# An attention and expert layer on one core: the output projection multiplied out earlier, small loads on another queue, norms, first front and maxima moved in the order

## The chip, the cores and the metric

The kernel runs on one core of one Trainium2 chip, in one launch. The metric is the device time in microseconds (us), the median of the runs. A core has a matrix engine (TensorE, in the profile PE, with its weight loads as PEld), a vector engine (VectorE, DVE), an activation engine (ScalarE, ACT), a general engine (GpSimd, POOL) and a sync engine (SyncE, SP) that here only issues DMAs. Every engine runs its own instructions in the order of the program and waits for the others by semaphores.

## The reference, cut to what matters

The input is 8 batches of 512 tokens of width 128, in f32. Two sublayers, each with a norm before and after, and a residual:

```
x = x + layernorm(attention(layernorm(x)))     # 1 head of 128, rotary, causal
x = x + layernorm(ffn(layernorm(x)))
# ffn(x):
h = rmsnorm(x, g1); c = h @ w_down             # 128 -> 64
q, k, v = rope(c @ wq), rope(c @ wk), c @ wv   # 16 heads of 4, causal softmax
x = x + attn @ w_up
t = rmsnorm(x, g2)
gate = top-2 of softmax(t @ router_w), 8 experts
y = sum_e gate_e * (silu(t @ w1_e) * (t @ w3_e)) @ w2_e     # all 8 experts computed
return x + y
```

The first attention has one head as wide as the model, the second has sixteen heads of width 4.

## The kernel before, in words

**Stages.** The program is one long order, written out by hand with generators: `yield` marks the places where pieces of two tasks are put side by side, and `step` advances a task by one piece. There are three stages: the wide attention (the first sublayer, batch by batch, to about 133 us), then the sixteen-headed attention in "units" of four heads (four units a batch, 32 in all), and the experts, from 441 us on. The next stage's first pieces are already mixed into the last batches of the stage before.

**The wide attention.** `wide_attention` goes through b = 0 to 8. In loop b it works on three batches at once: `norm` and `turn` of batch b + 1, `project`, `values` and `scores` of batch b, `turn_probs` and `weigh` of batch b - 1. It yields four times in a loop, so the i-th yield lies in loop i // 4. By engine:

- ACT: `norm` writes `xn` from `x_all` with a scale and shift of POOL's (L245); `turn` copies `xnT` from the matrix engine's bank (L256); `scores` takes exponentials into `p` (L299); `turn_probs` copies `pT` (L320); `values` copies `v` (L280).
- PE: `turn` transposes `xn` (L199), `project` makes `pq` (L262, one for q and one for k), `scores` makes `sc` in two halves with a mask added (L291, L292), `turn_probs` transposes `p` into `pT_ps` (L317), `values` makes `pv` (L272) and `weigh` makes `pr` (L327).
- DVE: two products `two` with the rotary table (L264), the row maxima `nmax` (L297), `h_all` (L336), the statistics of `x` (`stats_x`, tiles `bnst_x`), of the result (`norm_result`, `bnst_r`), the add of the normed result to `x_all` (`add`, L350), the statistics of that sum (`norm_sum`, `bnst_h`).
- POOL: the rotary sum `roped` (L266), which `scores` needs, the reciprocal roots (L169) and shifts.

`norm_result`, `add` and `norm_sum` run inside the loop for batches 0 to 2 (`CLOSED = 3`); the other batches' run later, by `close`.

On-chip accumulators: three double banks (`wide`, for `pq`, `sc`, and later `pqk`, `sm`, `sT`, `ph`) and, in this stage, two single banks (`bank`) that every transposition, `pv` and `pr` take by turns. A transposition into a bank waits until the copy of what was in it two turns before is done.

**Output projection.** Since the weights are fixed, `fuse_projections` multiplies `wv` by `wo` once, into `wvo`, and takes the row mean out of it, so that `values` gives values that are projected already: a transposition of `wv`, ACT's copy `wvT`, a product, three small DVE steps.

**Preparation.** `prepare` makes `wg` and `wqk4` from the second sublayer's small weights and turns its rotary table; `fill` writes constants and pads. They are stepped in loops 0 to 2 (list `setup`).

**The first front.** `ffn_front(b)` prepares batch b for the sixteen heads: POOL scales `x_all` into `hs` (L462), PE turns it into `hT_ps` (L199), then `pqk` (L534) and `pvs` (L546), a rotary product (L542) and sum `rot`, and POOL splits the result into three bf16 parts, `thirds` (L451 to L455). Six DMAs write them to DRAM (`q_dram`, `k_dram`, L569), and `load_rows` reads them back in another layout, `q_rows` and `k_rows`, with four DMAs (L577). For batches 0 and 1 SyncE issues these DMAs (`queue`). The front of batch 0 (list `first`) is stepped in loops 3 and 4, two pieces at a yield; that of batch 1 (list `fronts`) later, one piece at a time.

**Maxima.** Before a unit's weights can be computed, `rowwise` makes its scores by rows (`sm`, L617 and masks L600) and `highest` takes their maxima (`nm`, L632): six such blocks a unit, then POOL splits them into `m`, PE turns them (`m3T`, L650) and SyncE's six DMAs put them into `q_rows` (L658). `columnwise` then makes the scores by columns (`sT`, L673). `period(n)` is the order of one unit's time; it works on the maxima of unit n + 2. The maxima of units 0 and 1 are made in `period(-2)` and `period(-1)` (list `units_begin`, fourteen pieces), which are stepped in the last loops of the wide attention.

Of the kernel before, what the change touches and what calls it, by code (L numbers as in the profile page):

```python
# [8 lines left out]
F32 = mybir.dt.float32  # L9
BF16 = mybir.dt.bfloat16  # L10
# [5 lines left out]
P = 128  # L16
# [6 lines left out]
def kernel(  # L23
# [22 lines left out]
    nc = tc.nc  # L46
    B, T, D = x.shape
    NT = T // P
    L = w_down.shape[1]
    H, HD, HP = 16, 4, 32  # L50
# [3 lines left out]
    E, _, F = w1.shape  # L54
# [4 lines left out]
    const = ctx.enter_context(tc.tile_pool(name="const", bufs=1))  # L59
# [7 lines left out]
    def banks(stack, **bufs):  # L67

        for name, n in bufs.items():
            psum[name] = stack.enter_context(  # L70
                tc.tile_pool(name=f"ps_{name}_{n}", bufs=n, space=bass.MemoryType.PSUM)
            )
# [4 lines left out]
    def bank(name):  # L77
        return psum["bank"].tile([P, 512], F32, tag="bank", name=name)
# [3 lines left out]
    for b in range(B):  # L82
        nc.sync.dma_start(
            out=x_all[:, b * NT : (b + 1) * NT, :],
            in_=x[b].rearrange("(t p) d -> p t d", p=P),
        )
        if b == 0:
            ropea = const.tile([P, 2, T], F32, name="ropea")
            nc.sync.dma_start(out=ropea, in_=rope_a)


    wqk = const.tile([P, 2, 2, D], F32, name="wqk")
    for i, w in enumerate((a_wq, a_wk)):
        nc.scalar.dma_start(out=wqk[:, i, 0, :], in_=w[0])
        nc.scalar.dma_start(out=wqk[:, i, 1, 0 : D // 2], in_=w[0][:, D // 2 : D])
        nc.scalar.dma_start(out=wqk[:, i, 1, D // 2 : D], in_=w[0][:, 0 : D // 2])
    wv = const.tile([P, D], F32, name="wv")
    nc.scalar.dma_start(out=wv, in_=a_wv[0])
    wo = const.tile([P, D], F32, name="wo")
    nc.scalar.dma_start(out=wo, in_=a_wo[0])  # L100

    w1s = const.tile([P, E, F], F32, name="w1s")
    w3s = const.tile([P, E, F], F32, name="w3s")
    w2s = const.tile([P, E, FC, D], F32, name="w2s")
    for s in range(2):
# [4 lines left out]
            out=w2s[:, es, :, :], in_=w2[es].rearrange("e (c f) d -> f e c d", f=P)  # L110
# [71 lines left out]
    def ln_stats(src, n0, tag, n=NT):  # L182

        mv = moments(src, n0, tag, n)
        ve = stat.tile([P, n], F32, tag="ve", name=f"ve_{tag}_{n0}")
        nc.vector.tensor_scalar(ve, mv[:, :, 1], EPS, None, ALU.add)  # L186
        return mv, root(ve, tag)
# [20 lines left out]
    def fuse_projections():  # L208
        ps = bank("wvo_ps")
        nc.tensor.transpose(ps[:, :P], wv, ident)  # L210
        wvT = work.tile([P, D], F32, tag="sq", name="wvT", bufs=1)
        nc.scalar.copy(wvT, ps[:, :P])
        ps = bank("wvo_ps2")
        nc.tensor.matmul(ps[:, :P], wvT, wo, start=True, stop=True)
        mean = stat.tile([P, 1], F32, tag="wvo_mean", name="wvo_mean", bufs=1)
        nc.vector.tensor_reduce(mean, ps[:, :P], AX.X, ALU.add)
        nc.vector.tensor_scalar(mean, mean, 1.0 / D, None, ALU.mult)
        nc.vector.tensor_scalar(wvo, ps[:, :P], mean, None, ALU.subtract)

    def minus_product(a, b, tag, name):  # L220
        d = stat.tile([P, b.shape[1]], F32, tag=tag, name=name)
        nc.gpsimd.tensor_tensor(d, a, b, ALU.mult)
        nc.gpsimd.tensor_scalar(d, d, -1.0, None, ALU.mult)
        return d
# [3 lines left out]
    def stats_x(b):  # L228
        mv, rstd = ln_stats(x_all, b * NT, "x")
        x_stats[b] = minus_product(mv[:, :, 0], rstd, "shift_x", f"shift_x_{b}"), rstd  # L230
# [151 lines left out]
            h_scale[b] = kept  # L382

    batches = [Wide(b) for b in range(B)]
    with tc.manual_schedule():
        stats_x(0)
        batches[0].norm()
        stats_x(1)


    wdown = const.tile([P, L], F32, name="wdown")
    nc.gpsimd.dma_start(out=wdown, in_=w_down)
    wqkv = const.tile([L, 3, L], F32, name="wqkv")
    for i, w in enumerate((f_wq, f_wk, f_wv)):
        nc.gpsimd.dma_start(out=wqkv[:, i, :], in_=w)
    wup = const.tile([L, D], F32, name="wup")
    nc.gpsimd.dma_start(out=wup, in_=w_up)
    wr = const.tile([P, E], F32, name="wr")
    nc.gpsimd.dma_start(out=wr, in_=router_w)
    g1c = const.tile([P, 1], F32, name="g1c")  # L400
    nc.gpsimd.dma_start(out=g1c, in_=g1.rearrange("(p o) -> p o", o=1))
    g2c = const.tile([P, 1], F32, name="g2c")
    nc.gpsimd.dma_start(out=g2c, in_=g2.rearrange("(p o) -> p o", o=1))
    ropef = const.tile([P, NT, 2, HD], F32, name="ropef")
    nc.gpsimd.dma_start(out=ropef, in_=rope_f.rearrange("(t p) s d -> p t s d", p=P))
    ident_bf = const.tile([P, P], BF16, name="ident_bf")
    nc.vector.tensor_copy(ident_bf, ident)

# [3 lines left out]
        out=mask_a,  # L412
        in_=mask_a,
# [4 lines left out]
        channel_multiplier=1,  # L418
    )

    def half_masks(name, sign):


        m = const.tile([P, 2, P], BF16, name=name)
        nc.gpsimd.memset(m, 0.0)
        for i in range(2):
            for h in range(2):
                at = m[i * HR : (i + 1) * HR, h, :]
                nc.gpsimd.affine_select(
                    out=at,  # L430
                    in_=at,
                    compare_op=ALU.is_ge,
                    fill=NEG_BF,
                    base=sign * HR * h,
                    pattern=[[-sign, P]],
                    channel_multiplier=sign,
                )
        return m

    mask_q = half_masks("mask_q", -1)  # L440
    mask_k = half_masks("mask_k", 1)

    order = const.tile([P, E], F32, name="order")
    for e in range(E):
        nc.gpsimd.memset(order[:, e : e + 1], float(E - e))


    def split(thirds, x, r):
# [477 lines left out]
    fronts, backs, later = [], [], []  # L926

    def step(tasks):
        while tasks:
            try:  # L930
                next(tasks[0])
                return True
            except StopIteration:
                tasks.pop(0)
# [64 lines left out]
    def wide_attention():  # L999
        for b in range(B + 1):  # L1000
            u = batches[b] if b < B else None
            nxt = batches[b + 1] if b + 1 < B else None
            v = batches[b - 1] if b > 0 else None
            w = batches[b - 2] if 0 <= b - 2 < CLOSED else None
            if nxt:
                nxt.norm()
            if w:
                w.norm_result()
            if u:
                u.project(0)  # L1010
            if v:
                v.turn_probs(0, 1)
            if u:
                u.project(1)
            yield
            if b == 0:
                fuse_projections()
            if v:
                v.turn_probs(2)
                v.turn_probs(3)  # L1020
            if w:
                w.add()
            if u:
                u.values()
            if w:
                w.norm_sum()
            yield
            if v:
                v.weigh()
            if b + 2 < B:  # L1030
                stats_x(b + 2)
            if nxt:
                nxt.turn()
            if u:
                u.scores(0)
            yield
            if u:
                u.scores(1)
            yield

    def front_and_rows(b):
        yield from ffn_front(b)
        yield
        load_rows(b)

    CLOSED = 3
    setup = [prepare(), fill()]
    first = [front_and_rows(0)]
    units_begin = [period(-2), period(-1)]
    begun = period(0)  # L1050
    with tc.manual_schedule():
        banks(ctx, wide=3)
        with ExitStack() as stage:
            banks(stage, bank=2)
            batches[0].turn()
            fronts.append(front_and_rows(1))
            for i, _ in enumerate(wide_attention()):
                b = i // 4
                if b < 3:
                    step(setup)  # L1060
                    step(setup)
                elif b < 5:
                    step(first)
                    step(first)
                else:
                    step(first)
                    step(fronts)
                    if b > 5 or i % 4 > 1:
                        step(units_begin)
            for _ in range(6):  # L1070
                step(fronts)
                step(units_begin) or next(begun)
    closes = [batches[b].close() for b in range(CLOSED, B)]
    banks(ctx, bank=1, po=1)
    with tc.manual_schedule():
# [20 lines left out]
    for i, engine in enumerate((nc.gpsimd, nc.vector)):  # L1096
        n0, at = (B - 1) * NT + i * NH, slice(i * NH, (i + 1) * NH)
        st = ln_stats(h_all, n0, "o", NH)
        for t in range(NH):
# [3 lines left out]
            out=out[B - 1].rearrange("(t p) d -> p t d", p=P)[:, at, :], in_=y[:, at, :]  # L1103
# [71 lines left out]
```

## Time and profile before

| what | before |
|---|---|
| median of 3 runs | 798.55 us (798.25 to 801.8) |
| the profiled execution's own time | 799.5 us |
| its span, first to last instruction | 797.7 us |
| mean granted TensorE clock | 0.986 |
| PE busy | 726.2 us, 91% of the span |
| DVE, ACT, POOL busy | 490.3, 325.7, 285.1 us |
| DMA | 30.36 MB |

All times are those of one execution, taken by the profiler. A line of a timeline gives the start, the length, the engine, the program's line, the operation, the tile written and the tiles read, how many instructions were merged, and in brackets how long the engine was idle before it and what ended the idle time. SPq, ACTq and POOLq are the issue of DMAs. A line of the waits gives who waited for whom, the total in us, how many times, and the longest. A line of the windows gives the stretch, its length, the busy time of PE, PEld, DVE, ACT and POOL, the granted clock, the share of the DMA engines and GB/s. Matrix products run in a pipeline and their ends are modelled, so start-to-start distances are used for sums.

### The profile page before, as it was taken

How to read it: one execution, taken by the hardware profiler on the slowest of the kernel's cores; microseconds unless marked ns; L12 is line 12 of the kernel's file. 1: busy time of each engine (PE TensorE's matmuls, PEld its weight loads, DVE VectorE, ACT ScalarE, POOL GpSimd, SP SyncE). 2: the span in 40 equal slices, each digit the busy share in tenths (PEclk: the TensorE clock that was granted, in tenths of full speed). 3: DMA queues.
4: the chain of work that ended last, by engine and by line, in shares of the span. 5: the costliest groups of instructions: out<-in, count | busy, mean ns of one | idle time of the engine just before them, and what ended most of it. 6: DMA issues, size and time to landing. Idle time of an engine off the chain costs nothing. (4 is left out here: it accounts for less than half of the span.)

```text
span 797.7 us, 15024 instructions
## 1 busy us (share of the span) xinstructions
PE 726.2 (91%) x5886; PEld 433.0 (54%) x5886; DVE 490.3 (61%) x1090; ACT 325.7 (41%) x507; POOL 285.1 (36%) x595
## 2 busy tenths in 40 slices
PE   4989897898989889998899898999999999999995
PEld 2657465444445444544444455666666666666663
DVE  3587667788878777768672244746454545454554
ACT  2553533565656556656567323222222222222221
POOL 7576450456868676757424030101010101010101
PEclk9999999999999999999999899999999999999998
DMA  9121304040312122313000000000000000000000
GB/s 277 41 88 36 84 11 111 18 107 3 97 27 85 39 62 64 93 31 103 22 3 3 0 1 1 14 1 14 1 14 1 14 0 14 1 14 0 14 1 13
DMA packets 29017, 30.36 MB, mean 38 GB/s; under 512 B 6164, under 2 KB 25332, under 8 KB 28948
## 3 DMA queue, kind: packets, MB, share of 16 engines
q0 software_dynamic: 5280, 14.31, 7.0%
q1 hardware_dynamic: 22516, 14.72, 6.5%
q8 instruction: 46, 0.75, 0.4%
q10 hardware_dynamic: 1152, 0.39, 0.2%
q14 instruction: 23, 0.19, 0.1%
HBM read 15.73 MB, written 11.53 MB: 34 GB/s over the span
## 5 line engine op out<-in xcount | busy, mean ns | idle before, releaser
L632 DVE TENSOR_REDUCE nm<-sm 128x2 f32<-128x1024 f32 (+2 forms) x192 | 194.2, 1042 | 35.5 <-PE sm L600 30.6
L696 ACT ACTIVATE pk<-sT 128x1024 f32<-128x1024 f32 x160 | 161.2, 1024 | 78.5 <-PE sT L600 78.0
L874 ACT ACTIVATE sil<-ph 128x512 f32<-128x512 f32 x128 | 76.3, 597 | 248.4 <-PE ph L866 228.1
L875 DVE TENSOR_TENSOR hid<-sil,ph 128x512 f32<-128x512 f32 x128 | 87.2, 686 | 139.0 <-ACT sil L874 138.9
L887 PEld LDWEIGHTS py<-w2s,hid 128*128 128x128 f32 x1016 | 124.1, 193 | 33.4 <-issue 28.7
L866 PE MATMUL ph<-tT_all,w1s 128*128 128x512 f32 x256 | 131.9, 597 | 0.0
L866 PE MATMUL ph<-tT_all,w3s 128*128 128x512 f32 x256 | 131.1, 593 | 0.0
L887 PE MATMUL py<-w2s,hid 128*128 128x128 f32 x1016 | 125.2, 277 | 4.0 <-DVE o_nat L730 2.0
L169 POOL TENSOR_TENSOR root_o<-ve_o,half 128x4 f32<-128x4 f32 (+1 forms) x9 | 8.6, 951 | 295.4 <-DVE ve_o L186 259.9
L703 PE MATMUL po<-pk,vpad 128*32 128x512 f32 (+3 forms) x1024 | 97.8, 444 | 0.0
L896 DVE SCALAR_TENSOR_TENSOR h_all<-py,gate_all,h_all 128x128 f32<-128x128 f32 x254 | 71.7, 344 | 34.5 <-PE py L887 34.5
L866 PEld LDWEIGHTS ph<-tT_all,w3s 128*128 128x128 f32 x256 | 48.9, 191 | 61.8 <-issue 61.8
L673 PE MATMUL sT<-q_rows,k_rows 64*128 64x384 bf16 (+3 forms) x512 | 64.9, 299 | 18.2 <-DVE nm L632 13.8
L617 PE MATMUL sm<-k_rows,q_rows 61*128 61x256 bf16 (+3 forms) x512 | 71.1, 305 | 5.5 <-ACT pk L696 3.5
L866 PEld LDWEIGHTS ph<-tT_all,w1s 128*128 128x128 f32 x256 | 44.1, 192 | 31.7 <-issue 21.2
L617 PEld LDWEIGHTS <-q_rows 61*128 61x128 bf16 x512 | 23.5, 94 | 56.2 <-issue 52.1
L600 PE MATMUL sm<-ident_bf,mask_q 64*128 64x64 bf16 (+1 forms) x768 | 49.2, 200 | 0.0
L600 PEld LDWEIGHTS <-mask_q 64*128 64x128 bf16 x768 | 38.9, 96 | 12.0
L600 PE MATMUL sT<-ident_bf,mask_k 64*128 64x128 bf16 (+1 forms) x640 | 43.6, 206 | 0.0
L673 PEld LDWEIGHTS <-k_rows 64*128 64x128 bf16 x512 | 26.2, 93 | 31.6 <-issue 31.0
L451 POOL CAST m<-nm 128x16 bf16<-128x16 f32 x32 | 6.3, 198 | 88.0 <-DVE nm L632 88.0
L600 PEld LDWEIGHTS <-mask_k 64*128 64x128 bf16 x640 | 31.1, 94 | 11.2 <-issue 0.3
(174 smaller groups left out, 848.9 us busy)
## 6 DMA issues: line engine op xcount, KB each, us to landing
q_dram<-thirds POOLq DMA_DIRECT2D x18, 192.0 KB, 3.3
k_dram<-thirds POOLq DMA_DIRECT2D x18, 192.0 KB, 3.8
q_rows<-q_dram POOLq DMA_DIRECT2D x12, 288.0 KB, 4.9
k_rows<-k_dram POOLq DMA_DIRECT2D x12, 288.0 KB, 6.4
q_rows<-m3T SPq DMA_DIRECT2D x192, 2.0 KB
x_all<-in_L_attn_x_dram SPq DMA_DIRECT2D x8, 256.0 KB
out_dram<-y SPq DMA_DIRECT2D x7, 256.0 KB
q_dram<-thirds SPq DMA_DIRECT2D x6, 192.0 KB
```

The costliest lines, as they stand in the source:

```text
L169: nc.gpsimd.tensor_tensor(y, x, half[:, :n], ALU.pow)
L600: nc.tensor.matmul(out[:, :, h * HR : (h + 1) * HR], which[at, h, :], ident_bf[at, at].unsqueeze(1).to_broadcast([HR, out.shape[1], HR]), ...
L617: nc.tensor.matmul(sc[:, i, c * n : (c + 1) * n], self.q[at, 2 * self.g + pair, t * P : n], self.k[at, 2 * self.g + pair, :n], start=(c == 0),
L632: nc.vector.tensor_reduce(self.nm[:, :, pairs[0] : pairs[0] + w, t], sc[:, :, : w * n].rearrange("p i (c n) -> p i c n", n=n), AX.X, ALU.m ...
L673: nc.tensor.matmul(sc[:, i, c : c + n], self.k[at, 2 * self.g + pair, j * P : (j + 1) * P], self.q[at, 2 * self.g + pair, j * P :], start= ...
L696: nc.scalar.activation(p[:, :, :c], sc[:, :, :c], AF.Exp, scale=HD**-0.5)
L703: nc.tensor.matmul(po[h * HP : (h + 1) * HP, j * P :], vpads[self.g][:, j, h, :], self.p[j, h // 2][:, h % 2, :], start=(self.g == 0 and j ...
L866: nc.tensor.matmul(ph[:, i, :], w[:, e, c * P : (c + 1) * P], tT_all[:, b, :], start=True, stop=True,)
L874: nc.scalar.activation(sil, ph[:, 0, :], AF.Silu)
L875: nc.vector.tensor_tensor(hid[:, c, :], sil, ph[:, 1, :], ALU.mult)
L887: nc.tensor.matmul(py[:, t * P : (t + 1) * P], hid[:, c, t * P : (t + 1) * P], w2s[:, e, c, :], start=(c == 0), stop=(c == FC - 1),)
L896: nc.vector.scalar_tensor_tensor(h_all[:, n, :], (before if t < NT // 2 else py)[:, t * P : (t + 1) * P], gate_all[:, n, e : e + 1], h_all ...
```

## The change

The computation is the same; what changes is the order of instructions on each engine, and the queue that issues nine small loads:

- **Output projection.** `wv` and `wo` are loaded first on ACT's queue, ahead of `wqk`. `fuse_projections` is cut in two by a `yield`: the transposition of `wv` and its copy are placed before batch 0's `norm`, the product and the DVE steps after batch 0's `turn`. Before, all of it stood in loop 0 after the projections.
- **Small loads.** The nine loads of the second sublayer's small weights go from POOL's queue to SyncE's, behind the eight loads of `x_all` and ahead of the expert weights `w1s`, `w3s`, `w2s`.
- **Constants.** The masks `mask_q`, `mask_k` and the table `order` are written by POOL after the first `project` (`late_constants`), no longer ahead of it.
- **Wide norms.** In each loop `norm` of the next batch moves from the start of the loop to behind `turn_probs`, that is on ACT behind the exponentials and the copies of `pT`, and ahead of the copy of `v`.
- **Result and sum.** `norm_result` moves behind `turn_probs`, `norm_sum` runs one batch later (`summed`), and `add` moves to the end of the loop, behind the scores.
- **First front.** The list `first` is stepped in loops 4 and 5 instead of 3 and 4.
- **Maxima.** `units_begin` is stepped from yield 25 on instead of 22, and twice a yield in loop 8; `fronts` from loop 6 on instead of 5.

On DVE a batch's order becomes: `h_all`, statistics of `x`, `nmax`, `add`, two rotary products, result statistics, sum statistics, reciprocal. From the end of the stage on, PE's order is unchanged.

```diff
+    wv = const.tile([P, D], F32, name="wv")
+    nc.scalar.dma_start(out=wv, in_=a_wv[0])
+    wo = const.tile([P, D], F32, name="wo")
+    nc.scalar.dma_start(out=wo, in_=a_wo[0])
     wqk = const.tile([P, 2, 2, D], F32, name="wqk")
...
+    wdown = const.tile([P, L], F32, name="wdown")
+    nc.sync.dma_start(out=wdown, in_=w_down)
...
+    ropef = const.tile([P, NT, 2, HD], F32, name="ropef")
+    nc.sync.dma_start(out=ropef, in_=rope_f.rearrange("(t p) s d -> p t s d", p=P))
     w1s = const.tile([P, E, F], F32, name="w1s")
...
         nc.scalar.copy(wvT, ps[:, :P])
+        yield
         ps = bank("wvo_ps2")
...
     with tc.manual_schedule():
         stats_x(0)
+        projections = fuse_projections()
+        next(projections)
         batches[0].norm()
         stats_x(1)
-    wdown = const.tile([P, L], F32, name="wdown")
-    nc.gpsimd.dma_start(out=wdown, in_=w_down)
...
+        batches[0].turn()
+        next(projections, None)
...
+    def late_constants():
+        half_masks(mask_q, -1)
+        half_masks(mask_k, 1)
+        for e in range(E):
+            nc.gpsimd.memset(order[:, e : e + 1], float(E - e))
...
-            if nxt:
-                nxt.norm()
-            if w:
-                w.norm_result()
+            summed = batches[b - 3] if 0 <= b - 3 < CLOSED else None
             if u:
                 u.project(0)
             if v:
                 v.turn_probs(0, 1)
             if u:
                 u.project(1)
-            yield
             if b == 0:
-                fuse_projections()
+                late_constants()
+            yield
             if v:
                 v.turn_probs(2)
                 v.turn_probs(3)
             if w:
-                w.add()
+                w.norm_result()
+            if summed:
+                summed.norm_sum()
+            if nxt:
+                nxt.norm()
             if u:
                 u.values()
-            if w:
-                w.norm_sum()
             yield
...
             if u:
                 u.scores(1)
+            if w:
+                w.add()
             yield
...
-                elif b < 5:
+            elif b < 6:
+                if b > 3:
                     step(first)
                     step(first)
-                else:
-                    step(first)
-                    step(fronts)
-                    if b > 5 or i % 4 > 1:
-                        step(units_begin)
+            else:
+                step(first)
+                step(fronts)
+                if i > 24:
+                    step(units_begin)
+                if b == B:
+                    step(units_begin)
```

## The prediction

> **What bounds the kernel now.** Read first: the page's 40 slices. PE is busy nearly throughout, so work saved on another engine counts only where PE waits for it. The instruction order of PE is the same in both programs from the end of the wide attention on, so the change can act only before about 135 us, through PE's waits and its clock.
>
> ```profile
> PE   4989897898989889998899898999999999999995
> PEclk9999999999999999999999899999999999999998
> ```
>
> The digits are tenths, a slice is 20 us: the lower ones of the first seven slices are what can be won. Second: the waits of PE from 20 to 130 us.
>
> ```profile
> PE pT_ps L317 <- ACT pT L320: 5.2, 4, 1.6
> PE hT_ps L199 <- POOL hs L462: 1.3, 1, 1.3
> PE pT_ps L317 <- ACT p L299: 1.0, 2, 0.7
> ```
>
> The columns are total us, times, longest. The largest is the turned weights waiting for ACT to empty a bank. Third: PE's timeline at the first `ffn_front`, and the windows' row for the clock (the 1.00 or 0.50 before the last two columns).
>
> ```profile
> 54.06 0.66 PE L317 MATMUL pT_ps<-ident,p 128*128 128x128 f32 x4 [1.47 <-ACT pT L320]
> 54.56 1.06 PE L272 MATMUL pv<-wvo,xnT 128*128 128x128 f32 x8
> 56.95 1.64 PE L199 MATMUL hT_ps<-ident,hs 128*128 128x128 f32 x4 [1.34 <-POOL hs L462]
> 58.43 4.03 PE L327 MATMUL pr<-v,pT 128*128 128x128 f32 x20
> ```
> ```profile
> 59.00:60.00 1.00, 1.00 (x7) 1.00 (x7) 0.00 (x0) 0.22 (x1) 1.00 (x1) 0.50 0.07 16
> ```
>
> Two waits, four turns paced by POOL's `hs` (1.64 instead of 0.60), then 3.4 us at half clock: `pr` takes 4.03 where other batches take 2.40. Fourth: DVE's queue for one batch, in order, for its cost.
>
> ```profile
> 46.16 0.69 DVE L336 TENSOR_TENSOR h_all<-pr,rinv 128x512 f32<-128x512 f32 x1
> 46.77 0.86 DVE L177 BATCH_NORM_STATS2 bnst_x<-x_all 128x6 f32<-128x128 f32 x4
> 48.06 0.28 DVE L297 TENSOR_REDUCE nmax<-sc 128x1 f32<-128x128 f32 x1
> 51.22 0.86 DVE L177 BATCH_NORM_STATS2 bnst_r<-h_all 128x6 f32<-128x128 f32 x4
> 52.47 2.35 DVE L264 TENSOR_TENSOR two<-pq,ropea 128x1024 f32<-128x1024 f32 x2
> 54.74 2.30 DVE L350 SCALAR_TENSOR_TENSOR x_all<-h_all,root_r,x_all 128x128 f32<-128x128 f32 x4
> 56.96 0.86 DVE L177 BATCH_NORM_STATS2 bnst_h<-x_all 128x6 f32<-128x128 f32 x4
> 58.28 0.17 DVE L335 RECIPROCAL rinv<-sums 128x4 f32<-128x4 f32 x1
> ```
>
> Start to start: `h_all` 0.61, x statistics 1.29, four score maxima with ACT's exponentials between them 3.16, result statistics 1.25, two rotations 2.27, add 2.22, sum statistics 1.32, reciprocal 0.28: 12.4 us. PE's own work for a batch, from PE's timeline 34.00 to 45.74 without its waits: scores 2.55, projections 1.77 and 1.72, turns 0.33, 0.33 and 0.50, values 0.89, `pr` 2.28, turn 0.44: 10.8. Where a batch has all the DVE steps, DVE is the longer. Fifth: SyncE's timeline and PE's for the row loads.
>
> ```profile
> 76.40 0.60 SPq L569 DMA_DIRECT2D k_dram<-thirds  x1
> 81.73 1.67 SPq L577 DMA_DIRECT2D q_rows<-q_dram  x2
> 83.51 1.56 SPq L577 DMA_DIRECT2D k_rows<-k_dram  x2
> 90.98 0.39 PE L617 MATMUL sm<-k_rows,q_rows 61*128 61x512 bf16 x2
> ```
>
> POOL's `thirds` end at 76.37; the windows show the DMA engines busy until about 89.4; the first `sm` is at 90.98, with no wait. The chain takes 13.1 to 14.6 us and is just hidden.
>
> **The change, part by part**, on the clock of the profiled execution; sc(b) is the start of batch b's scores on PE (before: 21.00, 34.00, 45.74, 62.73, 76.44, 90.06 for b 0 to 5, and 120.40 for 7).
>
> *Start.* POOL issues no DMA (0.61 and 0.53) between root and shift, only a 0.30 select: shift at 7.35 instead of 8.12. ACT's table load ends at 7.48, then `wvT` 0.26: norm at 7.75, 0.4 earlier. While PE is slow at the start half of that is lost: `wdT` at 16.05. Before, PE then went through turn, product and three DVE steps until 19.57; now `wvo` is long done. But batch 1's norm (1.65) stands behind ACT's `wg`, which ends at 17.72: norm until 19.37, sc(0) at 19.6, 1.4 earlier.
>
> *Costed at nothing.* PE's queue now begins with the turn of `wv`, ahead of batch 0's turns; `wv` is ACT's first load (issue 0.73) and has until 8.2, where the first `x_all` landed by 3.99. `wqk` is issued two issues later (0.9 us) and has until 10.6. The nine small loads are issued from 9.05 at some 0.65 each (SyncE's small issues take 0.62): `g1c`, the seventh, at 12.95. POOL's took 5.2 to land, which would hold `wg` 0.8 too long; `q_dram` on SyncE is waited for 1.8; I take nothing and keep 0.8 for the range. `ropef`, at 14.25 with its 7.2, is there at 21.5, before its use. The expert weights behind them go out 5.9 later; their first use is at 441. The masks (3.45 of POOL) now stand behind the rotations and before `wqk4` (2.46) and the next shift (1.5): 18.65 to 26.1; POOL's next rotation comes at 26.8. If that cover is short, 1 us.
>
> *Norms behind the copies.* Of the four ACT waits, 0.77, 1.47 and 1.58 have a norm (1.64) ahead of the copy and go; so does 0.36 in batch 0's. The fourth, 1.36 at 127.12, has no norm before it and stays. ACT then does the norm while PE does values and `pr` (3.2), and the `v` copy still ends before the next turn. So sc(1) is 32.3 and sc(2) 32.3 + 10.8 = 43.1.
>
> *The add before the rotations.* Batch 2: `h_all` at sc(2) - 0.4, maxima over at +4.66, add at +6.88, rotations at +9.15, POOL's second sum at +10.65: PE wants it at +10.81. sc(3) = 53.9. But DVE then does two statistics and starts the next `h_all` only at +12.0, that is sc(3) + 1.2. Batch 3: maxima over at +6.26, add +8.48, rotations +10.75, POOL's sums +12.2.
>
> *The first front a batch later.* It leaves 62.73 (-1.34, -1.04 for the pacing, -1.63 for the clock) and comes back in batch 4's period: `hs` is queued on POOL behind those sums, from sc(3) + 12.2. PE is through with values at +8.95 and waits; behind its turns stand `pr`, the next turn and the scores. As before, `pr` starts 2.11 after `hs`: +14.3, a loss of 4.7, and I take the same 1.63 for the clock. sc(4) = 53.9 + 14.3 + 2.28 + 1.65 + 0.44 = 72.6. From there the old 13.71 (sc(3) to sc(4), which holds `pqk` and `pvs`): sc(5) = 86.3, still 3.8 ahead. If the turns are not held, 4.7 + 1.6 come back; if the add takes 3.40, as the row at 73.05 did beside POOL, 1 more.
>
> *The maxima moved.* `thirds` end: sc(4) + 6.43 for the maxima with `pqk`'s rotation, + 2.22 + 2.27, POOL + 1.43, split 1.9 = +14.25, 86.8. The rows land 13.1 to 14.6 later: 99.9 to 101.4. PE now meets the first `sm` after batch 6's values, 2.55 + 1.77 + 0.33 + 1.72 + 0.83 + 0.89 = 8.1 after sc(5): 94.4. It waits 5.5 to 7; I take 6.0 (the first `sm` needs only the first half's loads), and 1.7 for half clock. Behind it on PE: `pr`, turn, scores.
>
> *To the end of the stage.* sc(5) to sc(7) is 30.34 less 1.25 of waits; 1.7 of it (`pvs`, two `sm`) moves behind sc(7): 27.4. With 0.8 of waits: sc(7) = 86.3 + 27.4 + 6.0 + 1.7 + 0.8 = 122.2. Six `sm` blocks then share batch 7's end; the last maximum of unit 1 comes when `pr` is done (+10.3) plus `h_all` and two reduces, +12.7: 134.9. Before it ended at 133.4. Late by 1.5. On SyncE unit 1's six maxima rows now stand behind batch 1's row loads, which wait for their `q_dram`: another 0.5 at unit 1's `sT`.
>
> The rule of the Trainium skill that speaks against the change is TensorE: Matmul & The Clock Gate, Part 1: the clock is halved after an idle window of about 3.4 us, counted freely. The row above shows the half clock after idle stretches of only 1.47 and 1.34, so I follow the row. By the rule alone only the wait for the rows is sure to be punished, and the sum would be 1.6 lower.
>
> **Sum.** 799.5 (span 797.7 and 1.8 around it) + 2.0 = 801.5 for a profiled execution. That one was 0.95 above the median of 798.55: forecast 800.6.
>
> **Rivals.** (1) Forecast, 0.5: waits leave and return elsewhere. Own range 797 to 804. (2) Faster, 0.2: the rows are there in time because their chain is quicker on an otherwise quiet queue; without 6.0 + 1.7 it is 792.9, with half of it 796.7. For it: in before no part of the chain was pressed. Against: SyncE's six writes and four loads alone took 76.40 to 85.07 to issue. (3) Slower, 0.3: the wait for the rows is the whole chain and the clock stays half as long as at the start (8.7 to 14.4, 5.7 us). Place: the first `sm`. Price: 1.5 more wait, and 1.2 more clock at each of the two waits: 804.5. It decides from where the first `sm` starts over 15 us after sc(5). (4) The norms' move may not free the turns, if the copies then wait for the last exponential; at most 1 us, inside (1).
>
> **Numbers.** Range 793.5 to 806.5, from half of (2) to past (3) with the 0.8 and 1 us above. Half a per cent (4.0 us) is about what a measurement of this kernel can tell from no change. Faster by more takes nearly all of (2): 0.19; slower takes (3) and a tail of (1): 0.33; within: 0.48.
>
> **What would show it.** Right: first `sc` near 19.6; no PE wait on ACT's `pT` over 0.5 before 90; a wait of over 3 on `hs` near 63 to 67; one of about 6 before the first `sm`, with the clock at 0.50 after it. Wrong: `sm` starting within 10 us of sc(5); `hs` ready when PE arrives; or a later stage that takes a different length, which I hold to be unchanged.

## The result, and the profile after

| what | before | after |
|---|---|---|
| median of 12 runs each | 798.45 us | 805.0 us (802.6 to 810.12) |
| ratio, 95% interval | 1 | 1.008 (1.0059 to 1.0102) |
| profiled execution, span | 799.5, 797.7 us | 803.89, 802.1 us |
| mean granted TensorE clock, profiled | 0.986 | 0.976 |
| lost clock, median of runs | 9.6 us | 18.1 us |

The change makes the kernel slower, by 6.5 us or 0.8%. "Lost clock" is a quantity that the study needs: span times (1 - granted clock), the time that TensorE would have saved at most at full clock in that run (at most, since it also counts half clock during which TensorE waits, and the start). The lost clock of before is from the 35 runs beside the first four experiments (median 799.05). Time less lost clock, taken run by run, falls from 789.3 to 787.3 us: taken so, the new order by itself is 2 us shorter, and 8.5 us of clock are lost on top.

The slices of 20 us: the first seven digits of PE sum to the same 54 as before, and the clock's row has an 8 in the fourth, sixth, seventh and thirteenth slice, where before had a single one, at 440 to 460.

```profile
PE   5998797888989898989889898999999999999995
PEclk9998988999998999999999999999999999999998
```

PE's waits from 20 to 130 us (total, times, longest): three of the four waits for ACT's copies have gone, and a wait for the row loads is now the largest.

```profile
PE sm L626 <- DMA k_rows<-k_dram: 5.7, 2, 4.8
PE pT_ps L333 <- ACT pT L336: 2.2, 1, 2.2
PE hT_ps L214 <- POOL hs L471: 2.0, 1, 2.0
```

PE's timeline at batch 0's front and at the first maxima. Behind each wait `pr` takes 4.47 and 4.63 us, where the other batches' take 2.40 or 2.50, but for the last (3.79, at half clock behind the 2.2 us wait for `pT`).

```profile
64.30 1.78 PE L214 MATMUL hT_ps<-ident,hs 128*128 128x128 f32 x4 [2.02 <-POOL hs L471]
65.86 4.47 PE L343 MATMUL pr<-v,pT 128*128 128x128 f32 x20
...
92.04 1.16 PE L288 MATMUL pv<-wvo,xnT 128*128 128x128 f32 x8
98.01 0.51 PE L626 MATMUL sm<-k_rows,q_rows 61*128 61x512 bf16 x1 [4.81 <-DMA k_rows<-k_dram]
99.41 0.58 PE L626 MATMUL sm<-k_rows,q_rows 61*128 61x512 bf16 x1 [0.89 <-DMA k_rows<-k_dram]
...
100.03 4.63 PE L343 MATMUL pr<-v,pT 128*128 128x128 f32 x20
```

SyncE's timeline for the rows: the last five writes are issued from 84.68, the four loads from 89.69 to 93.0, and the first `sm` runs at 98.01. In before the first of these five went out at 76.40 and nobody waited.

```profile
84.68 0.62 SPq L578 DMA_DIRECT2D k_dram<-thirds  x1
89.69 1.66 SPq L586 DMA_DIRECT2D q_rows<-q_dram  x2
91.46 1.56 SPq L586 DMA_DIRECT2D k_rows<-k_dram  x2
```

DVE's queue in the same batch (first fence) and POOL's (second): the add is one block of 1.13 us and not 2.30, since POOL is idle beside it; `hs` stands behind the rotary sums on POOL.

```profile
58.95 1.13 DVE L366 SCALAR_TENSOR_TENSOR x_all<-h_all,root_r,x_all 128x128 f32<-128x128 f32 x4
60.00 2.35 DVE L280 TENSOR_TENSOR two<-pq,ropea 128x1024 f32<-128x1024 f32 x2
```
```profile
61.30 2.50 POOL L282 TENSOR_TENSOR roped<-two 128x512 f32<-128x512 f32 x2 [3.55 <-DVE two L280]
63.80 1.74 POOL L471 TENSOR_SCALAR hs<-x_all,h_scale 128x128 f32<-128x128 f32 x4
```

And the windows, this time of 3.41 us each (why that length, the last section tells): busy us of PE, PEld, DVE, ACT and POOL, then the clock. Here a stretch in which PE works for less than half (1.56 and 0.12 us of 3.4) is followed by two at 0.50.

```profile
57.17:60.58 3.41, 3.41 (x15) 1.88 (x14) 2.61 (x7) 2.29 (x7) 0.43 (x2) 1.00 0.00 0
60.58:64.00 3.42, 1.56 (x12) 1.13 (x10) 3.39 (x13) 3.04 (x7) 2.70 (x3) 1.00 0.00 0
64.00:67.41 3.41, 3.11 (x12) 2.37 (x13) 1.25 (x11) 0.59 (x1) 3.41 (x6) 0.50 0.00 0
...
94.72:98.13 3.41, 0.12 (x1) 0.09 (x1) 0.00 (x0) 0.00 (x0) 0.77 (x2) 1.00 0.59 151
98.13:101.54 3.41, 2.52 (x13) 1.82 (x13) 1.31 (x2) 0.00 (x0) 0.00 (x0) 0.50 0.01 2
101.54:104.96 3.42, 3.42 (x18) 3.42 (x18) 0.26 (x1) 0.00 (x0) 0.00 (x0) 0.50 0.00 0
```

### The profile page after: what moved, and what is told of

It is laid out like the page before. It is cut to its first block, busy times and chain, and to the rows that moved or that the text cites. A ratio compares the mean times of both kernels' runs of the same rounds, so it can differ in the third digit from the quotient of the medians.

```text
span 802.1 us, 15026 instructions
## 1 busy us (share of the span) xinstructions
PE 730.9 (91%) x5886; PEld 436.9 (54%) x5886; DVE 488.2 (61%) x1090; ACT 325.7 (41%) x507; POOL 280.0 (35%) x586
## 5 line engine op out<-in xcount | busy, mean ns | idle before, releaser
L905 DVE SCALAR_TENSOR_TENSOR h_all<-py,gate_all,h_all 128x128 f32<-128x128 f32 x254 | 71.7, 343 | 33.1 <-PE py L896 32.9
```

The costliest lines, as they stand in the source:

```text
L905: nc.vector.scalar_tensor_tensor(h_all[:, n, :], (before if t < NT // 2 else py)[:, t * P : (t + 1) * P], gate_all[:, n, e : e + 1], h_all ...
```

## The experiments

The theory after the first look: what the change gains at the start and at the copies is given back by the wait for the rows and by half clock behind every wait. The rival: one of the other parts (norms, small loads, output projection) costs the time. Experiments 1 to 4 take the change apart. "Time less lost" is the median of that difference, run by run; the ratio (to before, beside which each ran) is not the quotient of the two medians and differs from it by up to 0.0025. Runs 1 to 4, 5 to 8 and 9 to 10 are three groups, each beside its own runs of before (medians 799.05, 798.87 and 799.77), so across groups the ratio is the fairer comparison.

| run | median, us | ratio, 95% interval | lost clock | time less lost |
|---|---|---|---|---|
| 1 start only | 799.28 | 0.9997 (0.9963 to 1.0031) | 11.2 | 788.6 |
| 2 norms only | 799.9 | 0.9998 (0.9969 to 1.0026) | 11.6 | 787.3 |
| 3 front and maxima only | 807.37 | 1.0098 (1.0063 to 1.0133) | 14.9 | 791.1 |
| 4 all but front and maxima | 798.42 | 0.9995 (0.9969 to 1.0021) | 12.7 | 785.1 |
| 5 change, PE busy in the rows' wait | 803.4 | 1.0067 (1.0041 to 1.0092) | 14.4 | 789.1 |
| 6 change, maxima later | 795.23 | 0.9942 (0.9916 to 0.9968) | 16.7 | 778.7 |
| 7 change, add behind rotations | 803.35 | 1.0066 (1.0039 to 1.0093) | 14.4 | 788.9 |
| 8 as 4, PE busy in two waits | 794.36 | 0.9969 (0.9946 to 0.9991) | 9.1 | 785.8 |
| 9 as 6, PE busy in two waits | 792.37 | 0.9887 (0.9839 to 0.9935) | 8.7 | 782.8 |
| 10 as 9, add behind rotations | 793.27 | 0.9913 (0.9884 to 0.9942) | 9.5 | 783.7 |

**1, the start alone.** The change's diff for the output projection, the small loads and `late_constants`; all else as before.

```diff
-            if b == 0:
-                fuse_projections()
+        projections = fuse_projections()
+        next(projections)
         batches[0].norm()
...
-    nc.gpsimd.dma_start(out=wdown, in_=w_down)
+    nc.sync.dma_start(out=wdown, in_=w_down)
```

> Before, with only the start of the change: output projection multiplied out first, small loads by SyncE, masks behind the first projection; norms, front and maxima where they were. Theory (each part of the change moves the time by what it does to PE's waits and clock, and they add up): the first scores start at 18.4 instead of 21.0, and 2 to 2.6 us come off: 796.0 where before is 798.45. Rival (the start is hidden, because the row loads of the first front come no earlier): first scores early, but the gain is given back by the first sm: 798.5.

The first scores start at 19.44 instead of 21.00, and unit 1's `m3T` at 132.42 instead of 134.66. The waits for ACT's copies are all there. At the end nothing of the 2.2 us shows and the expected 796.0 did not come, though the interval is wide enough to hide it. In the profiled execution the stretch from unit 1's `m3T` to unit 31's takes it back: 297.5 us against 294.8 in before, with 10.2 us at half clock against 3.4.

```profile
PE pT_ps L333 <- ACT pT L336: 6.1, 5, 1.6
```

**2, the norms alone.**

```diff
-            if nxt:
-                nxt.norm()
...
                 v.turn_probs(3)
+            if nxt:
+                nxt.norm()
```

> Before, with only the wide norms moved behind the copies of pT. Theory: the ACT waits of 0.36, 0.77 and 1.58 go; the one of 1.47 is replaced by a longer wait for hs, which POOL finishes no sooner; PE comes to the first sm about as early as the rows land, so up to 1 comes back there: 796 to 797.5. Rival (the norm behind the copies makes the turn of the next batch late): 799 or more.

The waits for the copies fall from 5.2 to 1.4 us, as the change says; but PE comes to the front earlier, and the wait for `hs` grows from 1.3 to 2.7, with 6.8 us at half clock behind it (57.3 to 64.2). Unit 1's `m3T` is 1.3 us earlier, and the time is that of before, not the 796 to 797.5 expected.

```profile
PE hT_ps L199 <- POOL hs L462: 2.7, 1, 2.7
PE pT_ps L317 <- ACT pT L320: 1.4, 1, 1.4
```

**3, front, maxima, add, result and sum alone.**

```diff
-                elif b < 5:
-                    step(first)
-                    step(first)
+                elif b < 6:
+                    if b > 3:
+                        step(first)
+                        step(first)
...
-                    if b > 5 or i % 4 > 1:
+                    if i > 24:
+                        step(units_begin)
```

> Before, with only the first front, the maxima, the add, the result and the sum moved as in the change; start and norms as they were. Theory: this part alone is slower by more than the whole change, because the waits for hs and for the rows and the half clock behind them come without the gains: 807 to 811. Rival (the loss of the whole change comes from the start or the norms): 799 to 802.

This part alone brings the whole loss (0.98%): PE waits for the rows, then `pr` is slow. The profiled execution (802.02 us) is the fastest of the twelve, so its lines show the place of the loss and not its usual size.

```profile
98.24 0.37 PE L617 MATMUL sm<-k_rows,q_rows 61*128 61x512 bf16 x1 [3.55 <-DMA k_rows<-k_dram]
...
100.13 3.76 PE L327 MATMUL pr<-v,pT 128*128 128x128 f32 x20
```

**4, the change with the old front, maxima, add, result and sum** (that part of the diff taken back).

> The change without its moved front, maxima, add, result and sum: start and norms as changed, the rest as before. Theory: the two gains add up where the first sm does not take them back: 793 to 796. Rival (the loss is in the start or the norms): 802 or more.

Unit 1's `m3T` is at 131.05, 3.6 us earlier than before, and time less lost clock is 4.2 us shorter; lost clock is some 3 us more. Without the moved front the change is as fast as before, not slower; the expected 793 to 796 did not come either. The wait for `hs` shows how the clock takes it back:

```profile
55.23 1.79 PE L214 MATMUL hT_ps<-ident,hs 128*128 128x128 f32 x4 [2.73 <-POOL hs L471]
56.81 4.47 PE L343 MATMUL pr<-v,pT 128*128 128x128 f32 x20
```

So the part at fault is known: front and maxima, with the add, result and sum that moved with them. Open were two things: whether the front or the maxima cost it, and whether the price lies in the wait or in the clock.

**5, TensorE kept busy while the rows come.**

```diff
-            for t in range(NT):
+            for t in list(range(NT)) * (6 if self.b == 6 else 1):
                 nc.tensor.matmul(
                     pv[:, t * P : (t + 1) * P],
```

> The change whole, but batch 6's four value products are multiplied out six times in place, with the same result, so that TensorE works for some 4.5 us while the first row loads are on their way and is idle for about 1 us instead of 5.7. Theory (what the wait costs is mostly the half clock that follows it): the first sm stays near 98 to 99.5, since it is the DMA that sets it; no window at half clock between 98 and 105; pr of batch 5 takes 2.5 instead of 4.63 us; unit 1's m3T about 3 us earlier than 136.9; lost clock 3.4 us less over the whole, time about 802. Rival (the clock is cut by something other than the idle time, or the cut costs nothing because other engines set the pace behind it): the half clock stays, or it goes and unit 1's m3T stays at 136.9; time 805.

The first `sm` comes as the filler ends, at 98.23 (98.01 in after). The second still waits 1.32 for the rows and starts 14.7 us after sc(5), as in after (14.8), so it is the DMA that sets it. But `pr` takes 2.50 again, no window near 98 is at half clock, and unit 1's `m3T` is at 133.28 instead of 136.94.

```profile
92.62 5.62 PE L288 MATMUL pv<-wvo,xnT 128*128 128x128 f32 x48
98.23 0.37 PE L626 MATMUL sm<-k_rows,q_rows 61*128 61x512 bf16 x1
99.92 0.37 PE L626 MATMUL sm<-k_rows,q_rows 61*128 61x512 bf16 x1 [1.32 <-DMA k_rows<-k_dram]
...
100.28 2.50 PE L343 MATMUL pr<-v,pT 128*128 128x128 f32 x20
```

From sc(5) to sc(7) pass 33.1 us instead of 35.8: that much, 2.7, the clock behind this wait is worth. In the end 1.6 us show, which the intervals don't separate from nothing: this execution has half-clock stretches of its own at 135.0 to 138.4 and 145.2 to 152.1.

**6, the maxima three yields later.**

```diff
-                if i > 24:
+                if i > 27:
                     step(units_begin)
```

> The change whole, but the maxima of the first unit begin one stretch of four steps less early: from the steps of batch 7 on (i over 27) instead of from batch 6's (i over 24). Theory (the wait for the rows is what the moved front brought, and the price is the wait and its half clock): no wait for k_rows, no half clock near 98 to 105, sc(7) near 112 to 114 instead of 120.4; the maxima that are moved out (about 8 reduces of 0.6 to 1.2 us on VectorE) then stand behind sc(7) and take back 4 to 7 of the 8; time 799 to 803. Rival (the maxima themselves set the end of the stage and need to start at the latest when they do): unit 1's m3T later than 136.9, time 806 or more.

This is the run that decides. The rows are there when the first `sm` comes at 101.09, with no wait; unit 1's `m3T` is at 127.30, and the kernel beats before, and the 799 to 803 expected. Against the change, time less lost clock is 8.6 us shorter, more than the wait of 5.7; where the rest comes from was not followed. So the later front need not cost anything: with it, and with maxima that start after its rows are there, the kernel is faster than with the old front (0.9942 against 0.9995 in 4). The change moved the front by four yields and the maxima by three, here by six. The old front with later maxima was not run, so it is open how much of this gain needs the later front.

```profile
65.31 1.62 PE L214 MATMUL hT_ps<-ident,hs 128*128 128x128 f32 x4 [2.00 <-POOL hs L471]
66.77 2.40 PE L343 MATMUL pr<-v,pT 128*128 128x128 f32 x20
...
101.09 0.39 PE L626 MATMUL sm<-k_rows,q_rows 61*128 61x512 bf16 x2
```

The upper lines are a surprise: the same wait for `hs` as in the change (2.00 against 2.02), but `pr` is not slow. The windows show why: the idle time falls into two of the 3.41 us stretches, and in each PE works for 60% or more.

```profile
61.12:64.53 3.41, 2.06 (x16) 1.63 (x14) 3.38 (x11) 3.03 (x8) 2.20 (x2) 1.00 0.00 0
64.53:67.94 3.41, 2.32 (x15) 1.75 (x16) 1.73 (x12) 0.71 (x2) 3.41 (x7) 1.00 0.00 0
67.94:71.36 3.42, 3.42 (x24) 2.79 (x24) 2.05 (x11) 0.58 (x1) 1.82 (x4) 1.00 0.00 0
```

**7, the add behind the rotations.**

```diff
             summed = batches[b - 3] if 0 <= b - 3 < CLOSED else None
+            late = summed
...
             if u:
                 u.project(1)
+            if late:
+                late.add()
...
-            if w:
-                w.add()
             yield
```

> The change whole, but the sum of batch b-3 (add) stands behind the second projection of the next loop, that is behind both rotations on VectorE, where the change puts it before them. Theory (the 2.0 us wait for hs in front of batch 0's front, and the 6.8 us at half clock behind it, come from VectorE's queue of add and rotations): the rotations are 2.2 us earlier, PE's wait for hs is moved or shortened but POOL's sum comes later as well, so that the wait may return in another place; time 801 to 805. Rival (the order of add and rotations is indifferent, hs is bound by POOL's own queue): hs wait stays at 2.0, time 805.

The add takes 2.30 us again, beside POOL's `roped`, and the wait for `hs` is 1.49 instead of 2.02. The time is not to be told from the change's.

```profile
62.77 2.30 DVE L366 SCALAR_TENSOR_TENSOR x_all<-h_all,root_r,x_all 128x128 f32<-128x128 f32 x4
```

**8, experiment 4 with work for TensorE in two waits** (beside experiment 4's edit).

```diff
-            for t in range(NT):
+            for t in list(range(NT)) * (3 if self.b == 3 else 1):
...
             ps = psum["bank"].tile([P, 2, T], BF16, tag="bank", name=f"m3T_{self.name}_ps")
+            for _ in range(20 if self.b == 0 and self.g == 1 else 0):
+                nc.tensor.transpose(ps[:, 1, :P], ident_bf, ident_bf)
```

> The change without its moved front and maxima (start and norms only, as in the fourth run) and with filler for TensorE at two of its idle places: batch 3's value products are multiplied out three times in place (some 2.1 us of the 2.73 us wait for hs), and 20 transposes of the identity into an unused half of a bank stand before unit 1's m3T (some 1.1 us of the 1.61 us wait for m). The result is unchanged. Theory (half the clock lost behind those two waits is lost because TensorE stands idle): pr of batch 3 near 2.4 instead of 4.47 us, no or a shorter half clock at 55 to 62, sc(3) 3 us earlier than 61.9; the half clock at 133 to 138 gone; lost clock 4 to 7 us less than the fourth run's 12.7; time 793 to 796. Rival (the windows come in any case, or later ones take their place): lost clock unchanged, time 798 to 799.

`pr` of batch 3 takes 2.40 instead of 4.47, and from sc(2) to sc(3) pass 16.0 us instead of 18.6 although PE does 1.8 us more work, and the stretch at 133.7 to 137.1 is gone. So within the stage useless work makes the kernel faster: the clock is a cause of the time there and not a mark beside it. Other stretches at half clock stand elsewhere in this execution (121.5 to 124.9 and 152.2 to 155.6). Over the whole, lost clock falls by 3.6 us and the median by 4.1, but the two ratios to before (0.9995 and 0.9969) are only some 2 us apart and their intervals overlap, so that the whole kernel gains is not clear of the noise.

```profile
50.23 2.94 PE L288 MATMUL pv<-wvo,xnT 128*128 128x128 f32 x24
54.12 1.65 PE L214 MATMUL hT_ps<-ident,hs 128*128 128x128 f32 x4 [0.95 <-POOL hs L471]
55.60 2.40 PE L343 MATMUL pr<-v,pT 128*128 128x128 f32 x20
```

**9, experiment 6 with the same two fillers** (batch 4's value products instead of batch 3's).

> The change with the first unit's maxima from batch 7's steps on (as in the sixth run) and with the two fillers of the eighth: batch 4's value products three times in place (2.1 us, in the 2.00 us wait for hs) and 20 transposes of the identity before unit 1's m3T (1.1 us, in the 1.26 us wait for m). Result unchanged. Theory (the schedule without the wait for the rows is 8 to 9 us shorter than the change's, and what is left above it is half clock that follows TensorE's idle places): the half clock of 6.8 us at 125 to 133 goes or is 3.4, lost clock 9 to 13 instead of 16.7, time 788 to 792. Rival (windows come elsewhere instead, the sum stays): 794 to 796.

792.37 us over 6 runs, ratio 0.9887: the lowest median here, 1.1% under before; against experiment 6 the intervals overlap. Lost clock falls by 8.0 us against experiment 6, the time by 2.9 (4.4 by the ratios): time less lost clock is 4.1 longer. What takes that much back was not followed. The second filler came too late, as its row shows: PE was at half clock already (124.9 to 128.3), and 20 transposes took 2.32 us.

```profile
124.88 2.32 PE L660 MATMUL m3T_ps<-ident_bf 128*128 128x128 bf16 x20
127.13 0.30 PE L661 MATMUL m3T_ps<-ident_bf,m 128*48 128x128 bf16 x1
```

**10, experiment 9 with the add behind the rotations.**

> As the ninth run, and the sum of batch b-3 (add) behind the rotations as in the seventh. Theory (as in the seventh run the order of add and rotations moves the wait for hs by about 0.5 us and the rest of the stage by 1 to 2 earlier): unit 1's m3T 1 to 2 earlier than in the ninth run, time 787 to 791. Rival (indifferent, the seventh run's earlier m3T was a shorter half clock): same time as the ninth within 0.3%.

793.27 us, the same as 9 within the intervals; unit 1's `m3T` is later (129.94 against 127.13), not earlier. No effect of the order of add and rotations on the time is seen.

## Why the prediction was right, and where its sizes were off

The sign and the mechanism were right, and 805.0 lies in the range given, near its upper end; the forecast of 800.6 was 4.4 too low and its case "within 0.5%", to which it gave the highest chance, is not what happened. Of the 4.4, 2.4 lie in the profiled execution (803.89 against 801.5), and 2.0 in the 0.95 that the sum took off because before's profiled execution lay above its median: after's lies 1.1 below its own. Step by step, in the profiled execution of after:

| step | predicted | measured |
|---|---|---|
| sc(0), sc(1), sc(2), sc(3) | 19.6, 32.3, 43.1, 53.9 | 18.41, 31.50, 42.59, 53.68 |
| sc(4), sc(5), sc(7) | 72.6, 86.3, 122.2 | 70.91, 84.61, 120.36 |
| wait for `hs` | over 3 | 2.02 |
| wait for the rows | 6.0 | 5.7 |
| clock behind each of the two waits | one stretch of 3.4, worth 1.6 to 1.7 | two stretches, 6.8 |
| unit 1's `m3T`, against before | +1.5 | +2.28 |
| from there to unit 31's `m3T` | unchanged | +4.1 |
| end of the span | +2.0 | +4.4 |

**Start, norms, turns.** Right: no wait on ACT's copy of `pT` until the last batch; the fourth stays and is 2.2 instead of 1.36. The start gained 2.6 in this execution and not 1.4, but in the nine with the new start sc(0) lies between 18.09 and 20.18 (median 19.35), so 19.6 was well placed and the extra 1.2 is luck. The moved small loads, called nothing, show no wait on PE.

**The add.** Priced at 2.22 from a row in which POOL worked beside it; before the rotations, with POOL idle, it takes 1.13, and run 7 gives 2.30 behind them. `hs` starts 10.1 after sc(3) where 12.2 was worked out: 1.1 of that is the shorter add, and 1.0 that the add begins earlier (5.3 after sc(3) instead of 6.3). That is why the wait for `hs` came out shorter.

**The rows.** Right, down to the first `sm` 13.4 us after sc(5), where 14.1 was worked out. Rival (2), the rows in time, is excluded by the wait of 5.7; rival (3) needed over 15 us and did not get them, but its second half, the clock half for longer, is what came. Run 6 shows that the price of this step was larger than wait and clock: the change with its maxima later is 1.4%, some 11 us, faster than the change (0.9942 against 1.008), where the sum put 7.7 us on it.

**The clock.** This is the term that was mis-sized. The sum charged each wait one stretch of 3.4 us. The profile of after has two behind either wait, and runs 5 and 8 show that they cost time: 2.7 us behind the rows, against 1.7 in the sum. The number is not fixed, however. With the same order up to there and the same wait for `hs` (2.02, 2.01 and 2.00), two stretches stand behind it in after, one in run 5 and none in run 6: `pr` takes 4.47, 3.60 and 2.40, and from sc(3) to sc(4) pass 17.2, 16.0 and 14.7 us. Run 5's rows:

```profile
66.06 1.77 PE L214 MATMUL hT_ps<-ident,hs 128*128 128x128 f32 x4 [2.01 <-POOL hs L471]
67.62 3.60 PE L343 MATMUL pr<-v,pT 128*128 128x128 f32 x20
```

Up to unit 1 the short start and the short wait for `hs` paid for the two stretches, so the total there was off by only 0.8. That it came so close is luck.

**"A later stage that takes a different length, which I hold to be unchanged."** This is the step that failed. PE's order from there on is the same, but the clock is not. In after 13.6 us between 137 and 436 are at half clock (139.1 to 142.5, 190.3 to 193.7, 238.1 to 244.9), in before 3.4 (185.1 to 188.5): 6.8 against 1.7 us of TensorE's time, and the stage is 4.1 longer, as the windows from unit 1's `m3T` to unit 31's show (after, then before).

```profile
136.94:435.78 298.84, 265.41 (x3543) 139.01 (x3543) 224.84 (x340) 176.85 (x214) 185.60 (x415) 0.98 0.21 55
134.66:429.42 294.76, 261.16 (x3542) 137.44 (x3543) 224.67 (x340) 176.54 (x214) 184.63 (x415) 0.99 0.20 52
```

All twelve profiled executions say the same: this stage takes 294.8 to 300.3 us with 3.4 to 13.7 us of it at half clock, and less half of those it is 291.4 to 293.5 in every one. Before's execution has the least of the twelve, and runs 1, 2 and 4, with the old front, have 10.2, so not all of the 4.1 belongs to the change; how the 8.5 us of lost clock between the medians divide among the stages is open. On the other hand before has 6.8 us at half clock in the experts (451.4 to 458.2) and after none, which gives 2 us back.

**The rule on the clock.** The prediction followed the trace against the Trainium skill, TensorE: Matmul & The Clock Gate, Part 1, which halves the clock after an idle window of about 3.4 us. That choice was right: in after the stretch from 60.58 holds only 1.86 us of idle time and is followed by half clock. The page's other statement, that the window is 4096 cycles at 1.2 GHz, 3413 ns, and runs freely, was named in part ("counted freely") but nothing was drawn from it, and it would have helped. The trace agrees with it to the hundredth, see below.

## What to carry to other kernels

When a transfer that others wait for is started later, start those that wait later too: the moved front cost 1% with the maxima where they were put (run 3), and the change with them three yields later was 0.5% faster than with the old front (0.9942 in run 6, 0.9995 in run 4). Do not price a wait of a matrix engine by its length alone, and do not hold a later stage unchanged because its order is: count the half clock behind each gap as a range, and look at lost clock and time less lost clock separately. Where a gap can't be removed, harmless work in it can be worth more than it costs: 2.6 us in its stage in run 8. Over the whole kernel the three pairs with and without it (after and 5, 4 and 8, 6 and 9) point the same way, but none is clear of its intervals.

## What the runs showed of the hardware that was not expected

**Half clock comes on a grid.** In each of the twelve profiled executions (before, after, ten experiments) the stretches at half clock (but for the first 24 us and the end) start at one phase of a grid of 3.4133 us (in before 115 periods lie between the starts at 58.84 and 451.37): in before at 58.8, 127.1, 185.1 and 451.4, that is 0.23, 0.24, 0.23 and 0.25 of a period behind a multiple of it; in after 0.73 to 0.76; in the others other phases, each constant to about 0.03. They are 3.4 or 6.8 us long. The phase differs from one of these executions to the next.

**Half clock follows a low busy share of PE in one grid window.** Laid on each execution's own grid, 24 to 780 us, the windows at full clock give:

| busy share of PE in the window | windows | followed by half clock |
|---|---|---|
| to 0.505 | 39 | 37 |
| 0.506 to 0.62 | 57 | 20 |
| 0.62 to 0.72 | 58 | 1 |
| over 0.72 | 2416 | 0 |

A window that is itself at half clock is followed by another one whenever its share is under 0.84 (13 of 13). Busy shares rest on modelled ends of matmuls, so the limits are rough. They fit the study's puzzles: a gap of 2.0 us is punished when it falls into one window (after) and not when two share it (run 6), and an earlier change shifts which later gaps are punished. That the spread of the runs of one kernel (after: 802.6 to 810.12, at granted clocks of 0.980 and 0.969) has the phase as its cause is argued from this, not shown. What the runs do show is that the spread goes with the clock: over the 35 runs of before beside the first four experiments, a us more of lost clock goes with 0.8 us more of time (correlation 0.96).
